# A deformable convolution by tile products: the taps in reverse order, base rows outermost, and the columns that no output asks for left out

## The chip, the cores and the metric

The kernel runs on one core of a Trainium2 chip. The metric is the time on the device of one execution, in microseconds. Three executions of the kernel before took 1705.34, 1708.23 and 1708.29 us; the median is 1708.23.

## The reference

Eight images of 128 channels and 64 x 64 pixels go through two residual layers in fp32. The second layer (a mixture of 3x3 convolutions chosen by a gate) isn't touched by the change. The first is a modulated deformable 3x3 convolution on the group-normalised input, then batch normalisation, ReLU and the residual:

```python
om = lax.conv_general_dilated(x, off_w, (1, 1), ((1, 1), (1, 1)), ...) + off_b
off = om[:, :2 * KK].reshape(B_, KK, 2, H_, W_)      # an offset in y and x per tap and pixel
mask = jax.nn.sigmoid(om[:, 2 * KK:])                # a weight per tap and pixel
py = off[:, :, 0] + (row - 1.0) + ky
px = off[:, :, 1] + (column - 1.0) + kx
...
val = corner(y0, x0, (1 - ly) * (1 - lx)) + corner(y0, x0 + 1, (1 - ly) * lx) \
    + corner(y0 + 1, x0, ly * (1 - lx)) + corner(y0 + 1, x0 + 1, ly * lx)
out = jnp.einsum('bckhw,ock->bohw', val * mask, w)
```

For each output pixel and each of the nine taps one bilinear sample of every channel is taken at a position that the network itself predicts; the samples are weighted with the mask and summed over taps and channels.

## The kernel before

**Sampling as a matmul.** The kernel doesn't gather. It calls a position of the zero-padded 66 x 66 image a base position: output pixel (h, w) and tap (ky, kx) have base (h + ky, w + kx). Offsets are smaller than `REACH` = 2 pixels (a counter sends other inputs to a general path, which doesn't run here), so the sample of a base position is a weighted sum of the pixels within two of it. The base positions are cut into tiles of `T` = 6 by 6: 11 bands (`j`) of 11 tiles (`c`) an image, 88 bands and 968 tiles in all. A tile's samples, for all nine taps, come from a patch of 10 x 10 pixels, so they are one product: patch (100 pixels by 128 channels, transposed) times weights (100 pixels by 9 x 36 = 324 columns). A base position near the border belongs to fewer than nine pairs of pixel and tap: tap kx uses only the base columns kx to kx + 63, and likewise for rows.

**The steps of a tile**, each a small function in `dense()`:
- `weights(n)`, L542 to L552: VectorE multiplies the weights in x (`x_wts`) and in y (`y_wts`) of 100 pixels to `s`, 324 columns (L546). It runs three tiles ahead (`AHEAD`); `s` has five buffers.
- `sample(n)`, L554: TensorE multiplies the patch `xt` by `s` into `pq` (L557; an fp32 matmul appears in the trace as two instructions), and ScalarE copies `pq` into `samples`, which holds a band: nine taps, two rows of the band above and six of its own, 66 columns (L563). `pq` has three buffers.
- `conv(g - 1, i, py)`, L565: for the band before, one of nine taps of the convolution proper: TensorE multiplies 64 neighbouring columns of 6 rows of one tap's samples by that tap's 128 x 128 weights (L572; 384 columns, or 256 in the first band of an image), accumulating in `py`.
- `pixels(g + 1)`, L521: TensorE transposes the patches of the next band (L529) into `pt`, which has one buffer, and ScalarE copies them to `xt` (L536). `pick(g + 2)`, L503, copies the patches of the band after that out of the normalised image (L508, L516).
- `finish(g - 1, py)`, L579: bias, statistics and the store of the band.

**Order.** The schedule is written out by hand: in the loop of L640 each tile issues its step of every one of these, one step of the generator `tables(b + 2)`, and GpSimd's loads of weights for two bands ahead (`load_x` L485, `load_y` L471). At c = 1 ScalarE copies the last two rows of `samples` of the band above (L665). The first band issues no convolution.

**The tables.** `tables(b)`, L230, prepares an image: load, group norm (L257 to L286, with GpSimd's power L279 between), then the offset convolution, computed for pairs of rows. Sums of rows (`combos`, L312) are multiplied by weights derived from `offw_sb` by GpSimd (`offu_sb`, L612 to L616); the bias `offb_sb` is added at L351. Its 27 output rows go through HBM (`rowwise`, `colwise`) and come back with a base row, or a base column, on each partition: `off_y`, `mask` and `off_x`, views in `combos[1]`, each with nine taps of 66 or so columns (L393 to L411). Then, for each of five pixel distances, a tent function: in x on ScalarE (L453, L460), in y on VectorE (L458, L461, L463, the last one times the mask), and both are stored to the tables in HBM (L433, L441), which `load_y` and `load_x` read. For image 0 all of this runs ahead of the loop; for image 1 its loads are issued ahead, on the SP queue.

Of the kernel before, what the change touches and what calls it, by code (L numbers as in the profile page):

```python
# [8 lines left out]
F32 = mybir.dt.float32  # L9
# [7 lines left out]
P = 128  # L17
# [40 lines left out]
def deform_moe_conv(  # L58
# [110 lines left out]
    def dense():  # L169

        with ExitStack() as st:
# [15 lines left out]
            for t in picked:  # L187
# [16 lines left out]

            combos = [a1.tile([P, H // 2, W], F32, name=f"combo{i}") for i in range(2)]
            flat = combos[1].rearrange("p h w -> p (h w)")
            off_y, mask = (
# [2 lines left out]
                )  # L212
                for i in range(2)
            )
            off_x = flat[0:WB, 2 * YSTEP : 2 * YSTEP + TAPS * (WP6 - 1) + ROWPAD]


            x_wts = [a1.tile([P, NT1, T, TAPS, T], F32, name=f"xwts{i}") for i in range(3)]
            y_wts = [a1.tile([P, T, TAPS, WB], F32, name=f"ywts{i}") for i in range(2)]
            for t in (y_wts[0], x_wts[0]):  # L220
                nc.gpsimd.memset(t, 0.0)

            samples = [a1.tile([P, TAPS, T + 2, WB], F32, name=f"samples{i}") for i in range(2)]
            dw_sb = a1.tile([P, TAPS, P], F32, name="dw_sb")
            ystats = a1.tile([P, B, NT1, 6], F32, name="ystats")
            ymvs = a1.tile([P, B, 2], F32, name="ymvs")
# [3 lines left out]
            def tables(b):  # L230
# [160 lines left out]
                        nc.vector.memset(t, 0.0)  # L391
                yield from pause(9)
                for k in range(3):  # L393
                    rows = slice(k, k + H)
                    for t, c in ((off_y, 3 * k), (mask, 2 * TAPS + 3 * k)):
                        one = t[rows, 0, k, 0:1]
                        nc.sync.dma_start(
                            out=bass.AP(
                                tensor=one.tensor, offset=one.offset,
                                ap=[list(one.ap[0]), [3 * WB + 1, 3], [1, W]],  # L400
                            ),
                            in_=rowwise[b][c : c + 3].rearrange("s (h w) -> h s w", w=W),
                        )
                    one = off_x[rows, k * 3 * (WP6 - 1) + ROWPAD :]
                    others[k % 2].dma_start(
                        out=bass.AP(
                            tensor=one.tensor, offset=one.offset,
                            ap=[list(one.ap[0]), [WP6, 3], [1, H]],
                        ),
                        in_=colwise[b][k::3].rearrange("s w h -> w s h"),  # L410
                    )  # L411
# [3 lines left out]
                if b:  # L415
                    work = a1.tile([WB, 2, 2, YSTEP], F32, name="work", tag="om")
                    tents = [[work[:, a, i % 2] for i in range(NR)] for a in range(2)]
                else:
                    tents = []
                    for t in samples:  # L420
                        flat = t.rearrange("p k r w -> p (k r w)")
                        tents.append(
                            [flat[0:WB, i * YSTEP : (i + 1) * YSTEP] for i in range(NR)]
                        )
                one = off_x[:, ROWPAD:]
                by_bands = bass.AP(
                    tensor=one.tensor, offset=one.offset,
                    ap=[list(one.ap[0]), [T, NT1], [WP6 - 1, TAPS], [1, T]],
                )

                def store(i):
# [18 lines left out]
                for i in range(NR):  # L450
                    ty, tx = tents[0][i], tents[1][i]
                    step = steps[0:WB, i : i + 1]
                    nc.scalar.activation(  # L453
                        tx.rearrange("p (n k j) -> p n k j", n=NT1, j=T), by_bands, AF.Abs, bias=step
                    )

                    dy, at = off_y.rearrange("p u v j -> p (u v j)"), REACH - i
                    nc.vector.tensor_scalar(ty, dy, -1.0, float(1 - at), ALU.mult, ALU.add)  # L458
                    yield
                    nc.scalar.activation(tx, tx, AF.Relu, bias=1.0, scale=-1.0)  # L460
                    nc.vector.scalar_tensor_tensor(ty, dy, float(1 + at), ty, ALU.add, ALU.min)  # L461
                    yield
                    nc.vector.scalar_tensor_tensor(  # L463
                        ty, ty, 0.0, mask.rearrange("p u v j -> p (u v j)"), ALU.max, ALU.mult
                    )
                    if i:
                        store(i - 1)
                    yield from pause(2)
                store(NR - 1)

            def load_y(g, r, engine):  # L471

                if g >= len(bands):
                    return
                b, j = bands[g]
                engine.dma_start(  # L476
                    out=y_wts[g % 2][r * Q : (r + NR) * Q, r].rearrange("p b c -> p (b c)"),
                    in_=bass.AP(
                        tensor=y_table[b].tensor,
                        offset=y_table[b].offset + (T * j + r) * GROW + (NR - 1) * YSTEP,  # L480
                        ap=[[GROW - YSTEP, NR], [0, Q], [1, YSTEP]],
                    ),
                )
# [56 lines left out]
            def weights(n):  # L540

                if n >= len(bands) * NT1:  # L542
                    return
                g, c = divmod(n, NT1)
                s = a6.tile([P, TAPS, T, T], F32, name="s")
                nc.vector.tensor_tensor(  # L546
                    s[0:QQ],
                    x_wts[g % 3][0:QQ, c].rearrange("p a k r -> p k r a"),
                    y_wts[g % 2][0:QQ, :, :, T * c : T * c + T].rearrange("p r k a -> p k r a"),
                    ALU.mult,  # L550
                )
                ss[n] = s  # L552

            def sample(n):  # L554
                g, c = divmod(n, NT1)
                pq = ps_q.tile([P, TAPS, T, T], F32, name="pq")
                nc.tensor.matmul(  # L557
                    pq.rearrange("p k r a -> p (k r a)"),
                    lhsT=xts[g][0:QQ, c],
                    rhs=ss.pop(n)[0:QQ].rearrange("p k r a -> p (k r a)"),  # L560
                    start=True, stop=True,
                )
                nc.scalar.copy(samples[g % 2][:, :, 2 : T + 2, T * c : T * c + T], pq)  # L563

            def conv(g, i, py):  # L565


                b, j = bands[g]
                ky, kx = 2 - i // 3, i % 3
                n = 3 * kx + ky  # L570
                first = 0 if j else 2
                nc.tensor.matmul(  # L572
                    py[:, first:],
                    lhsT=dw_sb[:, 3 * ky + kx],
                    rhs=samples[g % 2][:, n, first + ky : T + ky, kx : kx + W],
                    start=(i == 0), stop=(i == TAPS - 1),
                )

# [14 lines left out]
            made, later = tables(0), tables(1)  # L593
            for _ in range(LOADS):
                next(made)
            nc.sync.dma_start(out=offw_sb[:, :, 0:27], in_=off_w)
            for j in range(4):
                nc.sync.dma_start(
                    out=offb_sb[32 * j : 32 * j + 27], in_=off_b.rearrange("a s -> s a")
                )  # L600
            def reach():

                near = a1.tile([P, B], F32, name="near")
# [36 lines left out]
            for g in range(len(bands) + 1):  # L640
# [8 lines left out]
                for c in range(NT1):  # L649
                    if g < len(bands):  # L650
                        n = g * NT1 + c
                        weights(n + AHEAD)
                        sample(n)

                        if c < 2:
                            load_x(g + 2, 2 * c, nc.gpsimd)
                            load_x(g + 2, 2 * c + 1, nc.gpsimd)
                        elif c < NT1 - AHEAD:
                            load_x(g + 2, c + 2, nc.gpsimd)
                        else:  # L660
                            for r in range(2 * (c - NT1 + AHEAD), 2 * (c - NT1 + AHEAD) + 2):
                                load_y(g + 2, r, nc.gpsimd)
                    next(ended, None)
                    if c == 1 and j:
                        nc.scalar.copy(  # L665
                            samples[g % 2][:, :, 0:2], samples[(g - 1) % 2][:, :, T : T + 2]
                        )
                    if g and c > 1:
                        conv(g - 1, c - 2, py)
                    next(turned, None)  # L670
                    for _ in range(1 + (c % 3 == 2)):
                        next(made, None)
                    if c == 5 and g + 2 < len(bands):
                        pick(g + 2)
                    if c == 7 and j == 1 and b:
                        nc.vector.bn_aggr(ymvs[:, b - 1], ystats[:, b - 1])
                    if c == 7 and (b, j) == (B - 1, 1):
                        reach()
# [566 lines left out]
```

## Time and profile before

| what | value |
|---|---|
| median of three executions | 1708.23 us |
| profiled execution, whole time | 1705.5 us |
| its span, first to last instruction | 1703.8 us |
| mean granted TensorE clock | 0.973 |
| TensorE busy | 1591.8 us, 93% |
| VectorE busy | 1280.1 us, 75% |
| ScalarE busy | 954.9 us, 56% |
| GpSimd busy | 938.3 us, 55% |
| first product of weights (L546) starts | 75.49 us |
| last matmuls of the first layer (L572) start | 1310.89 us |
| first matmul L1159 of the second layer starts | 1343.85 us |

How to read it: the span has a start of some 75 us, in which image 0 is loaded and its tables are built, then the loop over 88 bands to about 1311 us, then the second layer. Lines of groups, which follow, have the line, engine and operation, output and inputs with their shapes, the count, then busy time in us and the mean of one in ns, then how long that engine sat idle just before them and what it was waiting for. Lines of the timeline begin with the start and the duration in us, and x2 says that two instructions were merged. Ends of matmuls are modelled, so of matmuls the starts are to be used.

### The profile page before, as it was taken

What the parts mean: (1) busy time and instruction counts of PE and PEld (TensorE: products, weight loads), DVE (VectorE), ACT (ScalarE), POOL (GpSimd) and SP (SyncE); (2) the same over time, 40 slices, a digit from 0 to 9 for tenths busy, and PEclk for the clock granted to TensorE, in tenths of its full rate; (3) what the DMA queues carried; (4) which work ended last, traced back from release to release, by engine and by line L of the source; (5) the groups of instructions that cost most, each with busy time, mean ns of one, the idle gap of its engine ahead of it and who ended that gap; (6) DMA issues with size and microseconds to landing.
All of it is one profiled execution on the core that took longest, in us unless ns stands there. A gap on an engine that the chain in (4) does not pass through costs nothing. (4 is left out here: it accounts for less than half of the span.)

```text
span 1703.8 us, 20572 instructions
## 1 busy us (share of the span) xinstructions
PE 1591.8 (93%) x6106; PEld 918.3 (54%) x6106; DVE 1280.1 (75%) x1990; ACT 954.9 (56%) x1970; POOL 938.3 (55%) x1518
## 2 busy tenths in 40 slices
PE   3299999999999999999999999999999479999998
PEld 1155565666566556656665665566665234444443
DVE  6586777678687868776786878686664888888882
ACT  1465765776576667657765766676664423333320
POOL 3375576658667757766686676667771412222210
PEclk9599999999999999999999999999999689999999
DMA  4644864685477457647854775675762624444111
GB/s 133 128 119 113 166 169 114 143 183 132 112 159 183 115 120 184 154 114 141 192 125 110 161 183 126 129 162 133 171 149 53 266 87 155 158 153 149 76 63 52
DMA packets 197598, 235.82 MB, mean 138 GB/s; under 512 B 133964, under 2 KB 148048, under 8 KB 197478
## 3 DMA queue, kind: packets, MB, share of 16 engines
q0 software_dynamic: 94976, 124.94, 33.4%
q1 hardware_dynamic: 100556, 109.04, 21.6%
q8 instruction: 54, 0.88, 0.2%
q10 hardware_dynamic: 1946, 0.41, 0.1%
q14 instruction: 66, 0.54, 0.1%
HBM read 183.00 MB, written 50.82 MB: 137 GB/s over the span
## 5 line engine op out<-in xcount | busy, mean ns | idle before, releaser
L546 DVE TENSOR_TENSOR s<-xwts,ywts 100x324 f32<-100x324 f32 x968 | 706.6, 761 | 205.3 <-PE pq L557 172.3
L557 PE MATMUL pq<-s,xt 100*128 100x324 f32 x1936 | 693.5, 440 | 6.0 <-DVE s L546 6.0
L563 ACT COPY samples<-pq 128x324 f32<-128x324 f32 x968 | 425.1, 443 | 410.1 <-PE pq L557 403.5
L572 PE MATMUL py<-samples,dw_sb 128*128 128x384 f32 (+1 forms) x1584 | 624.4, 476 | 0.7 <-ACT y L583 0.7
L492 POOL DMA_DIRECT2D xwts<-tabx x863 | 524.7, 618 | 74.0 <-DMA ywts<-taby 35.9
L476 POOL DMA_DIRECT2D ywts<-taby x528 | 302.9, 588 | 337.2 <-DVE s L546 259.6
L557 PEld LDWEIGHTS pq<-s,xt 100*128 100x128 f32 x1936 | 324.5, 190 | 163.5 <-issue 28.7
L572 PEld LDWEIGHTS py<-samples,dw_sb 128*128 128x128 f32 x1584 | 299.9, 189 | 135.1 <-ACT y L583 2.7
L529 PE MATMUL pt<-ident,picked 128*100 128x128 f32 x968 | 194.6, 276 | 44.2 <-ACT picked L516 34.6
L529 PEld LDWEIGHTS pt<-ident,picked 128*100 128x100 f32 x968 | 121.0, 128 | 186.9 <-issue 44.8
L1159 PE MATMUL pc<-v,u 128*128 128x512 f32 x384 | 172.5, 598 | 9.3 <-DVE u L1108 9.3
L1159 PE MATMUL pc<-v,wmix 128*128 128x512 f32 x384 | 176.0, 604 | 0.0
L536 ACT COPY xt<-pt 100x512 f32<-100x512 f32 (+1 forms) x264 | 147.7, 559 | 2.2 <-PE pt L529 2.2
L1159 PEld LDWEIGHTS pc<-v,u 128*128 128x128 f32 x384 | 72.4, 190 | 98.3 <-issue 85.1
L1137 ACT ACTIVATE t<-pc,bmix 128x512 f32<-128x512 f32 x32 | 22.0, 687 | 182.3 <-PE pc L1159 100.3
L586 DVE BATCH_NORM_STATS2 ystats<-y 128x6 f32<-128x384 f32 (+1 forms) x88 | 48.3, 549 | 100.4 <-ACT y L583 100.4
L1159 PEld LDWEIGHTS pc<-v,wmix 128*128 128x128 f32 x384 | 72.3, 191 | 88.4 <-issue 84.7
L508 ACT COPY picked<-pad 128x900 f32<-128x900 f32 x88 | 91.6, 1041 | 9.6 <-DMA xwts<-tabx 9.6
L665 ACT COPY samples<-samples 128x1188 f32<-128x1188 f32 x80 | 95.9, 1199 | 0.0
L987 POOL TENSOR_TENSOR x<-x,xt 128x512 f32<-128x512 f32 x32 | 47.3, 1514 | 85.0 <-ACT x L985 85.0
L312 DVE TENSOR_TENSOR combo<-pad 128x1024 f32<-128x1024 f32 x64 | 77.4, 1227 | 8.5 <-PE pc L329 8.5
L987 POOL TENSOR_TENSOR pad<-pad,pad 128x512 f32<-128x512 f32 x28 | 39.6, 1445 | 71.7 <-ACT pad L985 71.5
(145 smaller groups left out, 998.3 us busy)
## 6 DMA issues: line engine op xcount, KB each, us to landing
ywts<-taby POOLq DMA_DIRECT2D x528, 116.0 KB, 4.2
pad<-in_x_dram SPq DMA_DIRECT2D x48, 512.0 KB
xwts<-tabx POOLq DMA_DIRECT2D x173, 116.0 KB, 4.1
out_dram<-yo SPq DMA_DIRECT2D x32, 512.0 KB
xwts<-tabx POOLq DMA_DIRECT2D x172, 92.8 KB, 4.0
yd<-y SPq DMA_DIRECT2D x80, 192.0 KB
xwts<-tabx POOLq DMA_DIRECT2D x173, 69.6 KB, 3.7
pad<-yd SPq DMA_DIRECT2D x16, 512.0 KB
```

What stands on the lines that cost most here:

```text
L476: engine.dma_start(out=y_wts[g % 2][r * Q : (r + NR) * Q, r].rearrange("p b c -> p (b c)"), in_=bass.AP(tensor=y_table[b].tensor, offset=y ...
L492: engine.dma_start(out=x_wts[g % 3][q:QQ:Q, :, lo:hi].rearrange("p t a b c -> p t (a b c)"), in_=bass.AP(tensor=x_table[b].tensor, offset= ...
L508: nc.scalar.copy(picked[g % 2][:, 1 : NT1 - 1], bass.AP(tensor=one.tensor, offset=one.offset, ap=[list(one.ap[0]), [T, NT1 - 2], [W, Q], [ ...
L529: nc.tensor.transpose(pt[0:QQ, c], picked[g % 2][:, c0 + c].rearrange("p y x -> p (y x)"), ident,)
L536: nc.scalar.copy(xts[g][0:QQ, c0 : c0 + n], pt[0:QQ, 0:n])
L546: nc.vector.tensor_tensor(s[0:QQ], x_wts[g % 3][0:QQ, c].rearrange("p a k r -> p k r a"), y_wts[g % 2][0:QQ, :, :, T * c : T * c + T].rear ...
L557: nc.tensor.matmul(pq.rearrange("p k r a -> p (k r a)"), lhsT=xts[g][0:QQ, c], rhs=ss.pop(n)[0:QQ].rearrange("p k r a -> p (k r a)"), star ...
L563: nc.scalar.copy(samples[g % 2][:, :, 2 : T + 2, T * c : T * c + T], pq)
L572: nc.tensor.matmul(py[:, first:], lhsT=dw_sb[:, 3 * ky + kx], rhs=samples[g % 2][:, n, first + ky : T + ky, kx : kx + W], start=(i == 0), ...
L665: nc.scalar.copy(samples[g % 2][:, :, 0:2], samples[(g - 1) % 2][:, :, T : T + 2])
L987: adder.tensor_tensor(y, y, xt[:, c * CH : (c + 1) * CH], ALU.add)
L1159: nc.tensor.matmul(pc, lhsT=us[j][:, kx], rhs=vs[g][:, rows, kx : kx + W], start=(kx == 0), stop=(kx == 2),)
```

## The change

The nine taps get a reversed order (the offset weights and their bias are loaded to a buffer and reversed by ScalarE copies), and all tables and samples are laid out so that a tile's 324 columns are, from outermost to innermost: base row, tap in y, base column, tap in x. With the reversed order the pairs of base position and tap that no output pixel uses are the first two or the last two of the 18 (row, tap in y) pairs in an edge band, and the first two or last two of the 18 (column, tap in x) pairs in an edge tile. The product and its copy leave these out there: 16 of 18 rows, 16 of 18 columns or both. `samples` has its four pairs that are never written set to zero once. The convolution now reads each tap's samples with a step of three elements. The tent in y is made in `combos[0]`, and its last step writes it in the new order; the tent in x reads its input in the new order. Other instructions keep their count.

```diff
+            tent_y = combos[0].rearrange("p h w -> p (h w)")[0:WB, 0:YSTEP]
...
-            x_wts = [a1.tile([P, NT1, T, TAPS, T], F32, name=f"xwts{i}") for i in range(3)]
-            y_wts = [a1.tile([P, T, TAPS, WB], F32, name=f"ywts{i}") for i in range(2)]
+            x_wts = [a1.tile([P, NT1, T, T, TAPS], F32, name=f"xwts{i}") for i in range(3)]
+            y_wts = [a1.tile([P, T, 3, WB, 3], F32, name=f"ywts{i}") for i in range(2)]
...
-            samples = [a1.tile([P, TAPS, T + 2, WB], F32, name=f"samples{i}") for i in range(2)]
+            samples = [a1.tile([P, T + 2, 3, WB, 3], F32, name=f"samples{i}") for i in range(2)]
+            for t in samples:
+                ends = t.rearrange("p r y w x -> p (r y) (w x)")
+                nc.gpsimd.memset(ends[:, 3 * T :, 0:2], 0.0)
+                nc.gpsimd.memset(ends[:, 3 * T :, 3 * WB - 2 :], 0.0)
...
-                    rows = slice(k, k + H)
+                    rows = slice(2 - k, 2 - k + H)
...
-                        one = t[rows, 0, k, 0:1]
+                        one = t[rows, 0, k, 2:3]
...
-                                ap=[list(one.ap[0]), [3 * WB + 1, 3], [1, W]],
+                                ap=[list(one.ap[0]), [3 * WB - 1, 3], [1, W]],
...
                 by_bands = bass.AP(
                     tensor=one.tensor, offset=one.offset,
-                    ap=[list(one.ap[0]), [T, NT1], [WP6 - 1, TAPS], [1, T]],
+                    ap=[list(one.ap[0]), [T, NT1], [1, T], [WP6 - 1, TAPS]],
                 )
...
                     nc.scalar.activation(
-                        tx.rearrange("p (n k j) -> p n k j", n=NT1, j=T), by_bands, AF.Abs, bias=step
+                        tx.rearrange("p (n j k) -> p n j k", n=NT1, j=T), by_bands, AF.Abs, bias=step
                     )
...
-                    nc.vector.tensor_scalar(ty, dy, -1.0, float(1 - at), ALU.mult, ALU.add)
+                    nc.vector.tensor_scalar(tent_y, dy, -1.0, float(1 - at), ALU.mult, ALU.add)
...
-                    nc.vector.scalar_tensor_tensor(ty, dy, float(1 + at), ty, ALU.add, ALU.min)
+                    nc.vector.scalar_tensor_tensor(
+                        tent_y, dy, float(1 + at), tent_y, ALU.add, ALU.min
+                    )
...
                     nc.vector.scalar_tensor_tensor(
-                        ty, ty, 0.0, mask.rearrange("p u v j -> p (u v j)"), ALU.max, ALU.mult
+                        ty.rearrange("p (v j u) -> p v j u", v=3, u=3),
+                        tent_y.rearrange("p (u v j) -> p v j u", u=3, v=3), 0.0,
+                        mask.rearrange("p u v j -> p v j u"), ALU.max, ALU.mult,
                     )
...
-                s = a6.tile([P, TAPS, T, T], F32, name="s")
+                s = a6.tile([P, 3 * T, T, 3], F32, name="s")
                 nc.vector.tensor_tensor(
                     s[0:QQ],
-                    x_wts[g % 3][0:QQ, c].rearrange("p a k r -> p k r a"),
-                    y_wts[g % 2][0:QQ, :, :, T * c : T * c + T].rearrange("p r k a -> p k r a"),
+                    x_wts[g % 3][0:QQ, c].rearrange("p a r (y x) -> p (r y) a x", x=3),
+                    y_wts[g % 2].rearrange("p r y a x -> p (r y) a x")[
+                        0:QQ, :, T * c : T * c + T
+                    ],
                     ALU.mult,
                 )
...
             def sample(n):
                 g, c = divmod(n, NT1)
-                pq = ps_q.tile([P, TAPS, T, T], F32, name="pq")
+                j = bands[g][1]
+                def asked(t, m0):
+                    m1, k0, k1 = m0 + 3 * T, 0, 3 * T
+                    if j == 0:
+                        m0 += 2
+                    if j == NT1 - 1:
+                        m1 -= 2
+                    if c == 0:
+                        k0 += 2
+                    if c == NT1 - 1:
+                        k1 -= 2
+                    return t[:, m0:m1, k0:k1]
+                pq = ps_q.tile([P, 3 * T, 3 * T], F32, name="pq")
                 nc.tensor.matmul(
-                    pq.rearrange("p k r a -> p (k r a)"),
+                    asked(pq, 0),
                     lhsT=xts[g][0:QQ, c],
-                    rhs=ss.pop(n)[0:QQ].rearrange("p k r a -> p (k r a)"),
+                    rhs=asked(ss.pop(n)[0:QQ].rearrange("p m a x -> p m (a x)"), 0),
                     start=True, stop=True,
                 )
-                nc.scalar.copy(samples[g % 2][:, :, 2 : T + 2, T * c : T * c + T], pq)
+                rows = samples[g % 2].rearrange("p r y w x -> p (r y) (w x)")
+                nc.scalar.copy(
+                    asked(rows[:, :, 3 * T * c : 3 * T * (c + 1)], 6), asked(pq, 0)
+                )
...
-                n = 3 * kx + ky
...
-                    rhs=samples[g % 2][:, n, first + ky : T + ky, kx : kx + W],
+                    rhs=samples[g % 2][:, first + ky : T + ky, 2 - ky, kx : kx + W, 2 - kx],
...
-            nc.sync.dma_start(out=offw_sb[:, :, 0:27], in_=off_w)
+            raw = combos[0].rearrange("p h w -> p (h w)")
+            raw_w = raw[:, 0 : TAPS * 27].rearrange("p (k s t) -> p k s t", s=3, t=TAPS)
+            raw_b = raw[0:1, TAPS * 27 : TAPS * 27 + 27].rearrange("p (s t) -> p s t", t=TAPS)
+            nc.sync.dma_start(out=raw_w.rearrange("p k s t -> p k (s t)"), in_=off_w)
+            nc.sync.dma_start(out=raw_b.rearrange("p s t -> p (s t)"), in_=off_b)
+            reversed_w = offw_sb[:, :, 0:27].rearrange("p k (s t) -> p k s t", t=TAPS)
+            offb_row = raw[0:1, TAPS * 30 : TAPS * 33]
+            reversed_b = offb_row.rearrange("p (s t) -> p s t", t=TAPS)
+            for k in range(TAPS):
+                nc.scalar.copy(reversed_w[:, :, :, k], raw_w[:, :, :, TAPS - 1 - k])
+            for k in range(TAPS):
+                nc.scalar.copy(reversed_b[:, :, k], raw_b[:, :, TAPS - 1 - k])
             for j in range(4):
-                nc.sync.dma_start(
-                    out=offb_sb[32 * j : 32 * j + 27], in_=off_b.rearrange("a s -> s a")
-                )
+                nc.sync.dma_start(out=offb_sb[32 * j : 32 * j + 27], in_=offb_row)
...
                         nc.scalar.copy(
-                            samples[g % 2][:, :, 0:2], samples[(g - 1) % 2][:, :, T : T + 2]
+                            samples[g % 2][:, 0:2], samples[(g - 1) % 2][:, T : T + 2]
                         )
```

The x offsets (`off_x`) come back in the reversed order too, and the views of `tents` and of `load_y` follow the new shapes.

More of the change, by code (lines that the diff above doesn't have):

```diff
@@ L403, in tables @@
                         )
-                    one = off_x[rows, k * 3 * (WP6 - 1) + ROWPAD :]
+                    one = off_x[rows, k * (WP6 - 1) + ROWPAD + 2 :]
                     others[k % 2].dma_start(
@@ L407, in tables @@
                             tensor=one.tensor, offset=one.offset,
-                            ap=[list(one.ap[0]), [WP6, 3], [1, H]],
+                            ap=[list(one.ap[0]), [3 * (WP6 - 1) - 1, 3], [1, H]],
                         ),
@@ L420, in tables @@
                     for t in samples:
-                        flat = t.rearrange("p k r w -> p (k r w)")
+                        flat = t.rearrange("p r y w x -> p (r y w x)")
                         tents.append(
@@ L476, in load_y @@
                 engine.dma_start(
-                    out=y_wts[g % 2][r * Q : (r + NR) * Q, r].rearrange("p b c -> p (b c)"),
+                    out=y_wts[g % 2][r * Q : (r + NR) * Q, r].rearrange("p a b c -> p (a b c)"),
                     in_=bass.AP(
```

## The prediction

> **What bounds the kernel now.** I read the page's parts 1, 2 and 5 first, then the table by stretches, then the timeline of TensorE in the middle of a band, and last the timeline of the start, because the chain of waits (part 4) only reaches back to the second layer and says nothing of the part that is changed.
>
> ```profile
> L546 DVE TENSOR_TENSOR s<-xwts,ywts 100x324 f32<-100x324 f32 x968 | 706.6, 761 | 205.3 <-PE pq L557 172.3
> L557 PE MATMUL pq<-s,xt 100*128 100x324 f32 x1936 | 693.5, 440 | 6.0 <-DVE s L546 6.0
> L563 ACT COPY samples<-pq 128x324 f32<-128x324 f32 x968 | 425.1, 443 | 410.1 <-PE pq L557 403.5
> L572 PE MATMUL py<-samples,dw_sb 128*128 128x384 f32 (+1 forms) x1584 | 624.4, 476 | 0.7 <-ACT y L583 0.7
> ```
>
> The two columns before the last say who waits: VectorE and ScalarE wait for TensorE (172 and 404 us), TensorE waits 6.0 us for the weights and 0.7 us for everything in the convolution.
>
> ```profile
> 320.00:480.00 160.00, 159.15 (x680) 97.72 (x679) 122.13 (x182) 106.31 (x231) 109.32 (x184) 1.00 0.66 146
> 480.00:640.00 160.00, 158.65 (x676) 97.30 (x675) 123.75 (x184) 107.46 (x233) 107.14 (x180) 1.00 0.65 144
> ```
>
> Columns: length, then TensorE, its weight loads, VectorE, ScalarE, GpSimd, granted clock, DMA share. TensorE is busy over 99% of these stretches at full clock; VectorE has 23%, ScalarE 33% free. Busy alone would not prove that it streams, so the starts:
>
> ```profile
> 603.98 0.71 PE L557 MATMUL pq<-s,xt 100*128 100x324 f32 x2
> 604.52 0.81 PE L572 MATMUL py<-samples,dw_sb 128*128 128x384 f32 x2
> 605.17 0.71 PE L557 MATMUL pq<-s,xt 100*128 100x324 f32 x2
> ```
>
> A product (two instructions of 324 columns) takes 604.52 - 603.98 = 0.54 us to the next start, a tap of the convolution (two of 384) 0.65 us. Finer, over several pairs of the timeline, 0.547 and 0.645: 0.098 us for 120 columns, or 0.82 ns a column. So from about 100 us to 1310 us each column left out of TensorE's stream is time off the end.
>
> **What the Trainium skill says.** "TensorE: Matmul & The Clock Gate", section "Back-to-back issue gap", gives columns/2.4 + 2.5 ns for a matmul; 2 x 384 columns at two passes each would be 645 ns by it, as the trace has. "SBUF — State Buffer", section "Door 1: The DMA port swizzle", says that reads are fastest where accesses hit the same 16-byte line ("need ≥2 hits per line to absorb SRAM access latency") and, in the same note, that a stride of up to 4 fp32 is free. For a step of 12 bytes (1.33 hits per line) the two halves disagree. The trace agrees that long steps cost: VectorE's s (first operand stepping 216 bytes) runs 7 back to back in 4.73 us, 2.09 ns an element. "PSUM — Partial Sum Buffer", section "Specifications (TRN2)", gives 8-byte lines and warns of non-contiguous outputs; the new output runs of 16 columns in rows of 18 start on even columns, so its pairs stay whole. The trace has outputs in runs of 63 (L329: 16 matmuls of 504 columns, four side by side, in 1.84 us from start to start, so 0.46 us for a set of four where streaming alone takes 504 x 0.82 ns = 0.41).
>
> **The change part by part.**
>
> *Columns left out (L557).* Of 11 tiles across two are edges, with 16 of 18 columns; of 11 bands down two are edges, with 16 of 18 rows. An image asks for (9x18 + 2x16)^2 = 194^2 = 37,636 columns in place of 198^2 = 39,204: 1,568 fewer, 12,544 for eight images, in two instructions each: 25,088 x 0.82 ns = 20.6 us. Band 0 (460 columns, 0.75 us) is not bound by TensorE, see below. Gain 19.8 us. The sample copies (L563) shrink with it on an engine that waits 404 us anyway: nothing.
>
> *The convolution's operand (L572).* Its 64 columns a row were neighbours, now they lie three floats apart. Count and columns stay. It streams 1,440 x 322 + 144 x 216 ns = 495 us in all. No matmul of the trace reads with a step, so I bound it: at best nothing. At worst a new line costs it twice the time of an element, as a long step does on ScalarE (L375, 256 bytes a step, 1.96 ns an element; L665, neighbours, 1,188 in 1.20 us, 1.01): four elements touch three lines, 6 for 4, 1.5 times, +247 us. I take nothing. The reason: an fp32 matmul takes its columns at 0.82 ns, two cycles of the 2.4 GHz that the TensorE page gives, so a new line on every element would still leave two of its own cycles per line, and the skill's stride sentence says 4 fp32 are free. It can't be a gain, since the matmul already runs at the rate of its columns.
>
> *The weights product (L546).* Its first operand stepped 216 bytes on each element; now it has runs of three. Counted the same way (two for a line touched, one for a further element on it), a run of three floats costs 3 or 4 by its alignment, 3.5 on average, against 6. At 2.09/2 ns each, 324 elements take 378 x 1.05 = 0.40 us, with what lies between two instructions some 0.5 us (an estimate) in place of 0.68 back to back. This is off the path but for the ramp (80 to 91 us): there VectorE is busy 10.35 of 11 us with s and L257 in turn, and TensorE only 9.41. 11 tiles x 0.18 us would be 2.0 us; I take 1.5 us gained, bounds 0 and 3.
>
> *Table building (L453 to L463).* L453 now reads with a step of 276 bytes, L463 reads both inputs with one of 792 bytes. At 2.09 ns an element 594 elements take 1.24 us, 1.3 with some bubble, for 0.77; ScalarE's transposing copy L375 (1,024 elements in 2.01 us) gives L453 594 x 1.96 = 1.17 us for 0.80. For images 1 to 7 this adds 35 x 0.53 = 19 us to VectorE, which s gives back many times over (968 x 0.18 us), and 35 x 0.36 = 13 us to ScalarE, out of some 50 us free in each 160: covered; without cover 32 us. Weights are made three tiles ahead (3.6 us), and three product buffers stand before ScalarE, so no single instruction of 1.3 us reaches TensorE. For image 0 nothing covers it:
>
> ```profile
> 49.26 0.46 DVE L458 TENSOR_SCALAR samples<-combo 66x594 f32<-66x594 f32 x1
> 49.75 0.77 DVE L461 SCALAR_TENSOR_TENSOR samples<-combo,samples 66x594 f32<-66x594 f32 x1
> 50.56 0.77 DVE L463 SCALAR_TENSOR_TENSOR samples<-samples,combo 66x594 f32<-66x594 f32 x1
> 51.25 0.46 DVE L458 TENSOR_SCALAR samples<-combo 66x594 f32<-66x594 f32 x1
> ```
>
> One step is 2.0 us, all VectorE, five steps, and the loads of band 0 wait for the last store. 5 x 0.53 = 2.6 us later (bounds 0 and 4). ScalarE's 1.17 + 0.70 = 1.9 us a step stays below the new 2.5.
>
> *Reversed offset weights (before L612).* Added: one more buffer, 18 ScalarE copies, and the four bias loads moved behind them, with dw_sb, db_sb and the next image's four loads queued after those on SP.
>
> ```profile
> 10.46 0.39 POOL L612 TENSOR_TENSOR offu_sb<-offw_sb 128x96 f32<-128x96 f32 x1
> 12.76 0.57 POOL L279 TENSOR_TENSOR scale<-ve,nhalf 128x1 f32<-128x1 f32 x1
> 13.56 2.93 ACT L285 ACTIVATE pad<-pad,shift,scale 128x512 f32<-128x512 f32 x4 [7.76 <-DVE shift L282]
> 15.39 4.63 DVE L312 TENSOR_TENSOR combo<-pad 128x1024 f32<-128x1024 f32 x4
> ```
>
> By its bytes the weight load lands near 9 us, behind image 0 on the DMA queues. Then, if the table load (1.28 us, now at 4.5) waits with the first copy, 9 copies of about 0.2 us (L516's 70 elements are 0.21 apart) end near 12.1. GpSimd runs L612 to L616 (2.2 us) to 14.3, and the scale (L279) queued behind it comes 1.5 us late, and with it shift, normalising and L312. The other nine copies end near 13.8, four bias loads take 2.5 us of SP (L598 now) and some 2 to land: 18 us. The combinations overwrite the buffer that these loads read, so L312, at 16.9 by then, waits 1.2 more. Together +2.7 us, bounds 0.5 and 5. dw_sb is first read at 90 us, image 1 at 82: both moved without effect. The four new GpSimd memsets (0.1 us each) lie in its wait.
>
> *Sum.* -19.8 + 2.7 + 2.6 - 1.5 = -16.0 us. The profiled execution took 1705.5 us (span 1703.8): 1689.5. The three runs have a median of 1708.2 and a mean of 1707.3, and I take 16 off the mean: **1691 us**. With the bounds (start 0.5 to 9, ramp 0 to 3, some of the column gain lost to jumps) its own range is 1684 to 1699.
>
> **Rivals.** (1) *The 12-byte step slows the convolution*: slower. Place: L572; price up to 247 us, 1938 us at 1.5 times; it decides from 16/495 = 3.2%, that is 333 ns a matmul in place of 322. For it: the two-hit rule and the 2 cycles a line of VectorE and ScalarE. Against it: TensorE's own rate of two cycles a column. Should it lie between, 10% gives 1740. (2) *The shortened products don't get shorter*, because 16 of 18 columns restart at each row: then only the start remains, 1707 + 3.8 = 1711. Against it: L329's runs of 63 are at most 0.05 us over their streaming. (3) *The gain is partly lost to other engines*: ScalarE's long table reads hold up xt, whose single PSUM buffer already costs TensorE 8.9 us (L529), and the start costs its upper bound: 1707 - 20 + 9 + 8 = 1704, no change that can be told.
>
> **How the numbers follow.** Forecast with its neighbours 0.70; rival 1 0.19, rival 2 0.04, rival 3 0.07. A measurement of this kernel tells about 0.2% (3.4 us) from no change, so faster 0.70, same 0.07, slower 0.23. Range 1682 to 1712: it holds the forecast, rivals 2 and 3 and the foot of rival 1, and leaves out most of rival 1 and little below. Both signs hold weight, so the likeliest case's own 1684 to 1699 stands beside it.
>
> **What will show it.** Starts of L572 pairs 0.645 us apart: step free; above 0.665, rival 1 wins. L557 in edge tiles 0.49 us to the next start, 0.43 in corners: columns are saved; 0.547: rival 2. Back-to-back s near 0.5 us. L463 near 1.3 us. The first s at about 81 us (75.5 now), L312 first at 18 (15.4 now). TensorE's busy share from 100 to 1290 us should stay over 99%; if it falls below, look for ScalarE (xt) as rival 3. A conv matmul that streams slower makes the prediction wrong at once.

## The result, and the profile after

The changed kernel takes 1953.68 us (median of four, 1953.48 to 1956.34), the kernel before 1707.89 in the same comparison: a ratio of 1.1446, 95% interval 1.1427 to 1.1466. The forecast was 1691; what came is the first rival, the 12-byte step of the convolution's operand. Its upper bound had been worked out as 1938; the measured time lies 16 us above even that.

The groups of the page of the changed kernel, same columns as before (L604 is the old L572, L559 the old L546, L594 the old L563, L587 the old L557):

```profile
L604 PE MATMUL py<-samples,dw_sb 128*128 128x384 f32 (+1 forms) x1584 | 911.1, 660 | 0.7 <-ACT y L615 0.7
L559 DVE TENSOR_TENSOR s<-xwts,ywts 100x324 f32<-100x324 f32 x968 | 461.2, 492 | 587.7 <-PE pq L587 549.3
L594 ACT COPY samples<-pq 128x324 f32<-128x324 f32 (+2 forms) x968 | 408.5, 423 | 648.2 <-PE pq L587 639.5
L587 PE MATMUL pq<-s,xt 100*128 100x324 f32 (+2 forms) x1936 | 675.3, 430 | 4.8 <-DVE s L559 4.8
```

The convolution's 1,584 instructions (two to a matmul) went from 624.4 to 911.1 us of busy time. ScalarE waits for TensorE 236 us more than before, VectorE 377. The weights product (L559) is a third shorter, and in the loop it bought nothing. The table by stretches (TensorE first, then its weight loads, VectorE, ScalarE, GpSimd):

```profile
320.00:480.00 160.00, 160.00 (x551) 84.68 (x550) 78.51 (x158) 94.91 (x198) 93.56 (x159) 1.00 0.53 131
480.00:640.00 160.00, 160.00 (x564) 80.83 (x564) 73.96 (x143) 88.20 (x184) 85.23 (x144) 1.00 0.51 122
```

TensorE is busy for all of it at full clock (1.00), with 551 instructions in a stretch that held 680: the time went into the single instruction, not into waiting. In TensorE's timeline the starts count:

```profile
604.62 0.72 PE L587 MATMUL pq<-s,xt 100*128 100x324 f32 x2
605.17 1.18 PE L604 MATMUL py<-samples,dw_sb 128*128 128x384 f32 x2
606.18 0.72 PE L587 MATMUL pq<-s,xt 100*128 100x324 f32 x2
...
616.37 0.65 PE L587 MATMUL pq<-s,xt 100*128 100x288 f32 x2
616.86 1.18 PE L604 MATMUL py<-samples,dw_sb 128*128 128x384 f32 x2
617.87 0.60 PE L587 MATMUL pq<-s,xt 100*128 100x256 f32 x2
618.31 0.38 PE L542 MATMUL pt<-ident,picked 128*100 128x128 f32 x2
```

The products do get shorter: 0.55 us to the next start with 324 columns, 0.49 with 288, 0.44 with 256. A pair (the two instructions of one matmul) of 384 columns of the convolution takes 1.01 us in place of 0.645: 1.32 ns a column and instruction, 1.57 times.

**The sum closes.** All numbers here are from the two profiled executions.

- The convolution: 80 bands of nine taps at 0.3675 us more (1.0125 is the mean of the pairs around this place) are 264.6 us, the eight short bands (0.67 for 0.44 us) 16.6: +281.
- The columns left out: 288 products 0.06 us shorter and 32 products 0.11 us: -20.8.
- TensorE's waits for the copies of `xt` between 100 us and the last band, summed from its timeline, go from 6.7 us to nothing: -6.7. (Where an expectation below has 7.9 us for the kernel before, one wait of 1.24 us is counted twice.)
- The start: the first weights product starts 0.9 us earlier (74.56 for 75.49), and the ramp (from there to the first matmul of the convolution) is 1.3 us shorter: -2.2.

Together +251.5. The trace has the same: the last block of the convolution starts at 1559.02 for 1310.89 and itself takes 3.4 us more, +251.5. The second layer, which isn't changed, was 3.7 us shorter in this execution, which gives the 247.8 between the two spans (1951.6 and 1703.8).

### The profile page after: what moved, and what is told of

Same layout as the page of the kernel before. It is cut to its first block, busy times and chain, and to the rows that moved or that the text cites. A ratio compares the mean times of both kernels' runs of the same rounds, so it can differ in the third digit from the quotient of the medians.

```text
span 1951.6 us, 20274 instructions
## 1 busy us (share of the span) xinstructions
PE 1853.1 (95%) x6106; PEld 934.7 (48%) x6106; DVE 1043.4 (53%) x1990; ACT 978.9 (50%) x1988; POOL 935.9 (48%) x1522
## 5 line engine op out<-in xcount | busy, mean ns | idle before, releaser
L604 PE MATMUL py<-samples,dw_sb 128*128 128x384 f32 (+1 forms) x1584 | 911.1, 660 | 0.7 <-ACT y L615 0.7
L559 DVE TENSOR_TENSOR s<-xwts,ywts 100x324 f32<-100x324 f32 x968 | 461.2, 492 | 587.7 <-PE pq L587 549.3
L594 ACT COPY samples<-pq 128x324 f32<-128x324 f32 (+2 forms) x968 | 408.5, 423 | 648.2 <-PE pq L587 639.5
L587 PE MATMUL pq<-s,xt 100*128 100x324 f32 (+2 forms) x1936 | 675.3, 430 | 4.8 <-DVE s L559 4.8
L587 PEld LDWEIGHTS pq<-s,xt 100*128 100x128 f32 x1936 | 332.1, 194 | 319.4 <-issue 226.8
L604 PEld LDWEIGHTS py<-samples,dw_sb 128*128 128x128 f32 x1584 | 300.0, 189 | 125.3 <-issue 5.0
L542 PEld LDWEIGHTS pt<-ident,picked 128*100 128x100 f32 x968 | 128.8, 134 | 268.6 <-issue 185.5
L542 PE MATMUL pt<-ident,picked 128*100 128x128 f32 x968 | 196.4, 277 | 37.2 <-ACT picked L529 35.0
L321 DVE TENSOR_TENSOR combo<-pad 128x1024 f32<-128x1024 f32 x64 | 76.9, 1218 | 17.8 <-PE pc L338 11.8
```

Source lines behind the costliest of these rows:

```text
L542: nc.tensor.transpose(pt[0:QQ, c], picked[g % 2][:, c0 + c].rearrange("p y x -> p (y x)"), ident,)
L559: nc.vector.tensor_tensor(s[0:QQ], x_wts[g % 3][0:QQ, c].rearrange("p a r (y x) -> p (r y) a x", x=3), y_wts[g % 2].rearrange("p r y a x - ...
L587: nc.tensor.matmul(asked(pq, 0), lhsT=xts[g][0:QQ, c], rhs=asked(ss.pop(n)[0:QQ].rearrange("p m a x -> p m (a x)"), 0), start=True, stop=True,
L594: nc.scalar.copy(asked(rows[:, :, 3 * T * c : 3 * T * (c + 1)], 6), asked(pq, 0))
L604: nc.tensor.matmul(py[:, first:], lhsT=dw_sb[:, 3 * ky + kx], rhs=samples[g % 2][:, first + ky : T + ky, 2 - ky, kx : kx + W, 2 - kx], sta ...
```

## The experiments

Each kernel is compared with the kernel before, run beside it on the same chip. That kernel's median lies between 1701.08 and 1706.83 us on the three chips used, so between chips only the ratios compare.

**The step alone.** Four kernels differ from the changed one in the convolution's operand: 64 floats of a row at another step. They read other samples than they should, so they compute something else, at the same count. All four also zero `samples` once, on GpSimd, and that had an effect of its own (see "with a clean start" below).

```diff
-                    rhs=samples[g % 2][:, first + ky : T + ky, 2 - ky, kx : kx + W, 2 - kx],
+                    rhs=samples[g % 2].rearrange("p r y w x -> p r (y w x)")[
+                        :, first + ky : T + ky, 2 * kx + 2 : 2 * kx + 3 + STEP * (W - 1) : STEP
+                    ],
```

> The changed kernel, but the convolution reads 64 neighbouring floats a row (other samples than it should: the output is not the reference's); its count, columns and weights stay. Theory A (the 12-byte step is the whole loss): an L572-like pair of 384 columns takes 0.645 us from start to start and the whole 1684 to 1692 us, 15 to 24 below the kernel before. Rival B (the new layout of samples itself, rows 2,376 bytes apart and written by ScalarE next to what is read, slows the convolution whatever the step): the pair stays near 1.01 us and the whole near 1950. Rival C (the step costs only part, and copies or weights cost the rest): in between, above 1720.

> As step1, but every second float (8 bytes). Theory L (a 16-byte line costs about 1.75 ns, and the matmul takes the longer of lines and columns): half a line a column, 0.875 ns against 0.84, a pair of 384 columns 0.67 us, the whole about 1710. Theory M (a line costs at least two columns' time, so two hits hide it): 0.645 us, the whole as step1. If any step at all costs: 1.0 us.

> As step1, but every fourth float (16 bytes, a new line each). Theory L: 1.75 ns a column, a pair 1.35 us, the whole about 2225. Theory M: 1.67 ns, a pair 1.28 us, the whole about 2180. If a stride of 4 fp32 is free, as the skill's sentence can be read, and only the odd step of three hurts: 0.645 us, the whole as step1.

> As step4, but every eighth float (32 bytes), so that every second 16-byte line is passed over. Theory L (each line that is touched costs about 1.75 ns, and nothing else counts): as step4, a pair of 384 columns 1.34 us, the whole 2215 to 2230. Rival D (the length of the step counts beyond 16 bytes, or it is a matter of banks): a pair of 1.5 us or more, or less than 1.2.

Measured: step1 1701.94 us (ratio 1.000, 0.999 to 1.001), step2 1727.96 (1.0151, 1.0121 to 1.018), step4 2221.57 (1.305, 1.3014 to 1.3087), step8 2241.51 (1.3174, 1.3131 to 1.3216). The starts of one pair in TensorE's timeline, step2 first:

```profile
706.25 0.86 PE L607 MATMUL py<-samples,dw_sb 128*128 128x384 f32 x2
706.94 0.65 PE L590 MATMUL pq<-s,xt 100*128 100x288 f32 x2
```

step4:

```profile
704.08 1.52 PE L607 MATMUL py<-samples,dw_sb 128*128 128x384 f32 x2
705.41 0.40 PE L545 MATMUL pt<-ident,picked 128*100 128x128 f32 x2
```

step8:

```profile
705.40 1.54 PE L607 MATMUL py<-samples,dw_sb 128*128 128x384 f32 x2
706.77 0.73 PE L590 MATMUL pq<-s,xt 100*128 100x324 f32 x2
```

| step in bytes | lines of 16 bytes per column | us a pair of 384 columns | ns a column | ns a line |
|---|---|---|---|---|
| 4 (step1b) | 0.25 | 0.645 | 0.84 | columns set the time |
| 8 | 0.5 | 0.69 | 0.90 | 1.80 |
| 12 (the change) | 0.75 | 1.01 | 1.32 | 1.76 |
| 16 | 1 | 1.33 | 1.73 | 1.73 |
| 32 | 1 | 1.37 | 1.78 | 1.78 |

A line here is 16 bytes of one partition's memory. Theory L holds within about 3%: a line costs about 1.75 ns, and a matmul takes the longer of its columns and its lines. At 8 bytes it gives 0.67 us, and 0.69 was measured; the whole, 1728, lies 11 us above its forecast once the 7 us of the start (below) are taken off. Theory M, whose 1.5 times had been my upper bound, gives 0.96 us for the change and 0.645 for step2; neither is what was measured. Rival D, as it was put (1.5 us or more, or less than 1.2), is out: twice the step adds 3% to the pairs shown, 1.5% to the mean instruction of all (862 ns for 849), and this rest stays unexplained. In the Trainium skill, "SBUF — State Buffer" (section "Door 1: The DMA port swizzle"), the sentence on two hits per line nearly agrees with the trace: at two hits (8 bytes) a pair takes 7% longer, at 1.33 hits (12 bytes) 57%. The reading of "4 fp32" as a step that is free does not agree: 16 bytes cost 2.06 times.

**The step alone, with a clean start.** step1 refuted theory A as written: 1702, not 1684 to 1692. Part of it was my own edit. Its timeline at the start:

```profile
13.99 8.05 POOL L291 MEMSET samples<- 128x4752 f32 x2
14.07 0.16 DVE L294 SCALAR_TENSOR_TENSOR shift<-gm,scale 128x1 f32<-128x1 f32 x1 [0.87 <-POOL scale L288]
14.27 2.93 ACT L297 ACTIVATE pad<-pad,shift,scale 128x512 f32<-128x512 f32 x4 [2.21 <-DVE shift L294]
14.27 9.42 DVE L298 TENSOR_SCALAR pad<-pad,scale,shift 128x512 f32<-128x512 f32 x4
```

The first of VectorE's four operations takes 8.06 us and ends only after GpSimd's zeroing, and everything of image 0 is some 7 us late (the first weights product starts at 81.3 us, for 74.56 in the changed kernel); so some 7 us are to be taken off the whole times of the four. step1b reads only written rows and zeroes nothing:

```diff
+                    rhs=samples[g % 2].rearrange("p r y w x -> p r y (w x)")[
+                        :, first + ky : T + ky, 2 - ky, 2 * kx + 2 : 2 * kx + 2 + W
+                    ],
```

> step1 without the two zeroings of samples by GpSimd, which kept VectorE's normalisation waiting (9.42 us for what takes 1.92) and made the first weights product start at 81.3 instead of 74.6 us; the convolution reads 64 neighbouring floats of the same rows, so the output is not the reference's. Theory A': all of the changed kernel's loss over this one is the step, and the columns' gain is partly taken back by waits for xt: the first s at 74.6 +- 0.5 us, 1694 to 1696 us. If the columns' gain is whole once the start is clean: 1685 to 1688.

step1b takes 1696.88 us, ratio 0.9946 (0.9927 to 0.9965). A pair, and the convolution as a whole, are back where they were before the change:

```profile
603.61 0.81 PE L604 MATMUL py<-samples,dw_sb 128*128 128x384 f32 x2
604.26 0.71 PE L587 MATMUL pq<-s,xt 100*128 100x324 f32 x2
```

```profile
L604 PE MATMUL py<-samples,dw_sb 128*128 128x384 f32 (+1 forms) x1584 | 625.6, 477 | 0.7 <-ACT y L617 0.7
```

The two kernels differ in nothing but which floats of a row the convolution reads, so the step costs 257 us (256 by the ratios), all of the loss, and rivals B and C of step1 are out. What is left of the change is 9 us faster than before, not 16 to 20. TensorE waits 17.5 us for the copies of xt (6.7 before), all of it before transposes, "<-ACT xt": that took back half of the columns' gain. The first weights product starts at 76.0 us, not at the expected 74.6, though up to there the program is that of the changed kernel. So a microsecond or two of a start differ between executions or chips, and smaller differences of the start mean nothing here.

**The same saving without the step.** With reversed taps the columns to leave out also stand first or last when tap in x lies outside of base column. So the samples of a tap can stay neighbours:

```diff
-            samples = [a1.tile([P, T + 2, 3, WB, 3], F32, name=f"samples{i}") for i in range(2)]
+            samples = [a1.tile([P, T + 2, 3, 3, WB], F32, name=f"samples{i}") for i in range(2)]
...
-                    x_wts[g % 3][0:QQ, c].rearrange("p a r (y x) -> p (r y) a x", x=3),
-                    y_wts[g % 2].rearrange("p r y a x -> p (r y) a x")[
-                        0:QQ, :, T * c : T * c + T
+                    x_wts[g % 3][0:QQ, c].rearrange("p a r (y x) -> p (r y) x a", x=3),
+                    y_wts[g % 2].rearrange("p r y x a -> p (r y) x a")[
+                        0:QQ, :, :, T * c : T * c + T
...
+                parts = [(slice(0, 3), slice(0, T))]
+                if c == 0:
+                    parts = [(slice(0, 1), slice(2, T)), (slice(1, 3), slice(0, T))]
+                if c == NT1 - 1:
+                    parts = [(slice(0, 2), slice(0, T)), (slice(2, 3), slice(0, T - 2))]
+                for xs, cols in parts:
+                    nc.scalar.copy(rows[:, :, xs, cols], made_of[:, :, xs, cols])
...
-                    rhs=samples[g % 2][:, first + ky : T + ky, 2 - ky, kx : kx + W, 2 - kx],
+                    rhs=samples[g % 2][:, first + ky : T + ky, 2 - ky, 2 - kx, kx : kx + W],
```

(`y_wts`, `off_y` and `mask` take the same order.) wide_full is this layout with all 324 columns everywhere.

> The same columns left out, but tap in x outside of base column, so that each tap's 64 samples of a row are neighbours; the weights product reads its first operand with 216 bytes a step again, the copies of edge tiles are two. Theory A: the convolution runs at 0.645 us a pair, the columns are saved, 1684 to 1693 us, so 15 to 24 below before. Rival (the saving in columns is not worth what I thought, or VectorE and ScalarE take it back): 1700 to 1710.

> The kernel called wide with all 324 columns in every tile: it is wide without the leaving out. If each column left out is time off the end: 20.6 us above wide, 1712. If TensorE then waits less for ScalarE's copies of xt, as the two gap lists (7.9 us in the kernel before, 13.9 in wide) suggest: 12 to 16 us above wide, 1704 to 1707.

wide: 1691.47 us, ratio 0.9934 (0.9912 to 0.9957), faster than both kernels, but by 10.5 us and not by the 15 to 24 expected. wide_full: 1710.83, ratio 1.0056 (1.0039 to 1.0074). The difference of the ratios, 1.22%, is 20.7 us; by the two intervals it lies between 16 and 26. The sum for all the columns was 20.6 (19.8 without band 0). In the two profiled executions the last block starts 17.3 us earlier in wide (1300.38 for 1317.67): 20.6 less the 2.9 us that TensorE waits more for xt there (13.9 for 11.0). So the columns left out do come off the end, and part may go again into waits; these two runs can't tell 17 from 21.

But the layout itself costs 9.5 us (7 to 13 by the interval). TensorE's waits for xt account for 4.3 of it (11.0 in wide_full for 6.7) and slightly longer convolution matmuls (627.4 us busy in wide_full, 624.4 before) for about 3; the rest is open.

**Who makes TensorE wait.** ScalarE's timeline in wide, where TensorE stands still from 499.8 to 501.05 us for the copy of xt:

```profile
497.57 0.77 ACT L469 ACTIVATE work<-work 66x594 f32<-66x594 f32 x1
498.17 0.83 ACT L603 COPY samples<-pq 128x324 f32<-128x324 f32 x2
498.81 1.48 ACT L462 ACTIVATE work<-combo,steps 66x594 f32<-66x594 f32 x1
500.10 0.53 ACT L603 COPY samples<-pq 128x216 f32<-128x216 f32 x2
500.42 0.58 ACT L548 COPY xt<-pt 100x384 f32<-100x384 f32 x1
```

and TensorE's at the same place:

```profile
501.05 0.43 PE L541 MATMUL pt<-ident,picked 128*100 128x128 f32 x2 [1.21 <-ACT xt L548]
```

The copy stands in line behind L462, which reads with a step of 276 bytes and takes 1.43 us (0.82 before). Two kernels change the order of L462's reads and writes alone: wide_abs has neither step, which gives weights that belong to other taps and rows, so it computes something else at the same count; wide_wr reads neighbours and steps on the write. One changes the PSUM buffers of the transposed patches (pt) and the products. Two try to bring back the short weights product, one of them with VectorE as the copier of xt:

```diff
-                    ap=[list(one.ap[0]), [T, NT1], [1, T], [WP6 - 1, TAPS]],
+                    ap=[list(one.ap[0]), [T, NT1], [WP6 - 1, TAPS], [1, T]],
...
# wide_abs writes in that order too; wide_wr writes tx by "p (n j k) -> p n k j"
...
# wide_q2t2: ps_q with 2 buffers for 3, ps_t with 2 for 1
# wide_fast: s written by "p m x a -> p m a x", its inputs as in the changed kernel
# wide_fast_xt: wide_fast, and
-                    nc.scalar.copy(xts[g][0:QQ, c0 : c0 + n], pt[0:QQ, 0:n])
+                    nc.vector.tensor_copy(xts[g][0:QQ, c0 : c0 + n], pt[0:QQ, 0:n])
```

> wide, but the tent in x reads and writes in the order of the kernel before (its weights then belong to other taps and rows: the output is not the reference's). Theory E (ScalarE's table activation, 1.40 us since it reads with a step of 276 bytes, 0.82 before, holds up the copies of xt): TensorE's gaps fall from 13.9 to about 8 us, the whole to 1683 to 1687. If the shorter stream of the edge tiles alone makes the gaps, whatever that activation takes: gaps stay above 12 us, the whole 1690 to 1692.

> wide, but the tent in x reads neighbours and writes with a step of 36 bytes instead; it computes the same. If ScalarE's stepped writes are cheaper than its stepped reads: L462 below 1.0 us and the time of wide_abs. If they cost the same, as VectorE's did in wide_fast: 1.4 us and the time of wide, 1690 to 1693.

> wide with two PSUM buffers for the transposed patches (pt) and two instead of three for the products (pq). If the single buffer pt is what the gaps hang on: gaps below 6 us, 1680 to 1686. If ScalarE's lateness only moves to the products (L586 then waits for the copies of samples): 1690 or more.

> wide, but the weights product reads its first operand in runs of three, as in the changed kernel, and writes with a step of 24 bytes. If a stepped write is free: s 0.49 us in place of 0.76, the whole 1688 to 1692, since VectorE isn't what ends the bands. If a stepped write costs as a stepped read: s stays above 0.7 us. The gaps of TensorE before the transposes (13.9 us) stay, since ScalarE makes them.

> wide_fast, and VectorE, not ScalarE, copies the transposed patches (xt). If ScalarE's bursts (two table activations and a picked copy in a row) are what holds the single buffer pt: the 13.9 us of gaps fall below 4, the whole 1677 to 1682. If it is the one buffer itself, whoever copies: gaps stay above 10 and the whole at 1688 to 1692.

| kernel | us | ratio to before (95%) | TensorE's waits, 100 us to the last band |
|---|---|---|---|
| wide_abs | 1684.49 | 0.9862 (0.9828 to 0.9897) | 7.4 |
| wide_wr | 1691.54 | 0.9907 (0.9871 to 0.9942) | 13.4 |
| wide_q2t2 | 1699.46 | 0.9944 (0.9923 to 0.9965) | 13.4 |
| wide_fast | 1700.04 | 0.9991 (0.998 to 1.0002) | 15.9 |
| wide_fast_xt | 1700.24 | 1.0002 (0.9985 to 1.0019) | 14.3 |

In wide_abs, and then in wide_wr, the group of that activation and the group of the transposes, whose last number is TensorE's whole wait for xt:

```profile
L462 ACT ACTIVATE work<-combo,steps 66x594 f32<-66x594 f32 x35 | 28.8, 821 | 6.8 <-DMA tabx<-work 6.6
L541 PE MATMUL pt<-ident,picked 128*100 128x128 f32 x968 | 195.1, 277 | 44.4 <-ACT picked L528 34.4 <-ACT xt L548 9.7
```

```profile
L462 ACT ACTIVATE work<-combo,steps 66x594 f32<-66x594 f32 x35 | 48.8, 1395 | 1.0 <-DMA tabx<-work 1.0
L541 PE MATMUL pt<-ident,picked 128*100 128x128 f32 x968 | 195.4, 277 | 50.4 <-ACT picked L528 34.3 <-ACT xt L548 15.7
```

Theory E holds: with the short activation the waits for xt fall to 7.4 us, and the whole is 7.1 us below wide_wr on the same chip (1681.78 to 1685.93 us in four executions, for 1689.14 to 1694.46). ScalarE's stepped write costs what its stepped read does (1,395 and 1,432 ns). A second pt buffer takes away every wait of the transposes for xt, but a product buffer paid for it: in wide_q2t2 TensorE waits as long in sum for the copies of samples, as this line of its timeline shows:

```profile
195.79 0.81 PE L586 MATMUL pq<-s,xt 100*128 100x324 f32 x2 [1.28 <-ACT samples L603]
```

That wide_q2t2 is also 7.9 us slower than wide_wr on the same chip, with the same sum of waits, stays open. VectorE as the copier doesn't help either (L542 then waits 11.3 us for VectorE's xt), and wide_fast_xt's 1700 us lie outside both of its forecasts. Nor did wide_fast do what I wanted: with a stepped write s takes 750 ns. That it is 0.57% slower than wide (9.7 us by the ratios, on another chip) is only partly told: its first weights product starts 2.9 us later and TensorE waits 2.0 us more for xt; the rest is open.

## Why the prediction was wrong, by its own steps

- **The step that failed**: the term "The convolution's operand (L572)", put at nothing ("I take nothing"). Two reasons were given: that two of TensorE's cycles a column (0.82 ns) leave enough time for a new line on every element, and that the Trainium skill's sentence ("SBUF — State Buffer", section "Door 1: The DMA port swizzle") makes a step of 4 fp32 free. Both failed. The runs show about 1.75 ns a line, more than two columns' time (1.64), so 0.75 lines a column outlast the column; and a step of 4 fp32 takes 2.06 times. The upper bound (1.5 times, +247 us) was near the size and somewhat low: 1.57 times, +281 us in the convolution and 257 in the whole; of the 24 us between, 17.5 are waits for xt that step1b has and the slow convolution hides. The case was named and priced; it was given 0.19. The trace before held the better clue: ScalarE and VectorE paid about 2 ns for each new line, and nothing in it showed that TensorE reads another way.
- *What bounds the kernel* was right: TensorE's stream, before and after.
- *Columns*: right. 0.55, 0.49 and 0.44 us a product, 20.8 us in all by these starts.
- *Weights product*: right in the main. Back to back it takes 0.42 us (six in 2.52 us, in the line below) for "some 0.5", in place of 0.68; one alone takes 492 ns. The band without convolution got 1.3 us shorter for the 1.5 predicted; what the columns left out there did of it was not separated.
- *Table building*: both sizes off. L474 (L463 before) takes 830 ns, not 1,300, so a step of image 0 takes 2.18 us, and 0.9 us were lost over its five steps, not 2.6. L462 takes 1,402 ns, not 1,170.
- *Reversed weights*: +2.7 us predicted, nothing lost that can be told. ScalarE's table load went to 0.79 us, ahead of the wait, nine copies took 1.36 us, the bias's nine 0.96, so the scale kept its place (12.79 for 12.76 us) and L321 started 0.5 us late, which later steps made up. The first weights product of the changed kernel:

```profile
74.56 2.52 DVE L559 TENSOR_TENSOR s<-xwts,ywts 100x324 f32<-100x324 f32 x6 [17.09 <-DMA ywts<-taby]
```

- *"No single instruction of 1.3 us reaches TensorE"* was wrong as well: pt has one buffer, and a longer L462 ahead of its copy does. In the changed kernel the slow convolution hides this. In the layout of wide it costs about 7 us (wide_wr less wide_abs), which is rival 3's mechanism. For the change without the step (step1b, 1696.88) the 1691 is some 6 us too low, and that it comes so near is in part luck: 10.8 us of added waits for xt had been put at nothing, and most of the 5.3 us that the start was to lose did not come.

## What to carry to other kernels

Before an operand of a matmul is laid out with a step, count the 16-byte lines per column: in fp32 neighbours touch 0.25 and are free, 8 bytes touch 0.5 and made the matmul 7% longer, 12 bytes touch 0.75 and made it 1.57 times as long. If a saving needs an order of columns, look for another order with the same saving that keeps the busiest reader's elements adjacent (here tap outside of column did), and let an engine with slack take the step, unless the bound engine waits for something behind it: ScalarE was a third idle, and its stepped tent still cost 7 us. A faster stage on the bound engine leaves the other engines less time to answer (TensorE's waits for xt: 11.0 us in wide_full, 13.9 in wide): look at single-buffered tiles first.

## What the runs showed of the hardware

- An fp32 matmul's moving operand (here the samples, which stream past the weights) costs about 1.75 ns for each 16-byte line it touches, where that is longer than its columns' 0.84 ns each; 32 bytes a step cost at most 3% more than 16 (table above). Longer steps were not run.
- A step on VectorE isn't always dear: L474 reads both inputs with 792 bytes a step, three elements at a time, in 830 ns for 771 without a step, while s with six elements at 216 bytes on one input takes 760 for the 492 it takes in runs of three. No run here tells why.
- GpSimd zeroing 2 x 4,752 floats (8.05 us) held a VectorE tensor_scalar with its operands elsewhere: four took 9.42 us for 1.92. The Trainium skill, "SBUF — State Buffer", section "Who interferes with whom", has such a lock between the two for VectorE's two-port modes; the trace agrees as far as it goes (the mode can't be seen in it).
